# Parity-and-pair order for residuals, results and biases, and a second copy of the first layer's result, in a two-layer hypernetwork convolution

## The chip, the core and the metric

The kernel runs on one core of a Trainium2 chip. The metric is the device time in microseconds of one execution. Before the change it is 4303.06 us, the median of 3 runs (4301.34 to 4310.08). The profile is of one further execution, which took 4305.81 us; its span from the first to the last instruction is 4303.7 us.

## The reference

Two layers of the same form follow each other. Each normalizes its input by groups, computes a weight for every position from a small network on `z`, convolves with it (3 taps), adds a bias from a second network, and adds the input back:

```python
S2, B, CI, CO, L, K, A, H = (32, 32, 64, 64, 256, 3, 16, 128)
h = jax.nn.relu(_ln(z @ W1 + b1, g1, be1))
w = (h @ W2 + b2).reshape(B, L, CI, CO, K)
hb = jax.nn.relu(_ln(z @ Wb1 + bb1, gb1, beb1))
bias = (hb @ Wb2 + bb2).transpose(0, 2, 1)
x_uf = jnp.stack([xp[..., i:i + L] for i in range(K)], axis=-1)
out = jnp.einsum('sbilk,bliok->sbol', x_uf, w) + bias[None]
# twice:
x = x + conv(_gn(x), z, W1, b1, ...)     # x: (32, 32, 64, 256), f32
```

`_gn` splits the last axis (256 positions) into 32 groups of 8 and normalizes over everything but the first axis (32 samples) and the group. So the second layer can't normalize before the first has finished for all 32 images `b`.

## The kernel before, in words

A *unit* `u` is one image `b` of one layer: 0 to 31 are layer 1, 32 to 63 layer 2. A *half* `v = 2u + h` is 32 of its 64 output channels. The main loop runs over the 128 halves.

In a half, `make` (L384) computes twelve pieces of weights, each 16 matmuls `pg <- hT, w2t` (L391, L392); `take` (L395) adds `b2` and moves them into `wall` on DVE (L402) and, for a third of the rows, on ACT (L417). After the first `make` of a half come the `products` (L424) of the half before: 320 short matmuls `pc <- wall, xn` (L434) in four groups `q` of 16 of the 64 positions of a quarter `t`, each group added to the residual by DVE (L443) and, in layer 1, followed by two calls of `bn_stats` (L446) for the next layer's groups. PSUM holds two `pc`. Then `after` (L464) queues what follows a half: `store` of the result, `load_residual` of `v + 2`, `normalize` of half the samples of a coming unit on GpSimd (two steps, L381), the next `load_pairs`, `add_bias` (L362, GpSimd) for `v + 1` and `load_bias` for `v + 2`.

`room` holds `xt`, the buffer for pairs, and `ys`, a ring of three residuals. "Pairs" is the layout that the convolution reads: partition = parity of the position and input channel (2 x 64), free = sample and pair (128). The input `x` lies in DRAM twice: as `xs` (partition = quarter of the positions and sample, 4 x 32; free = output channel and position) for residuals and statistics, and as `xp` in pairs. The first layer's result lies in DRAM once, as `x1[u]`, channel x sample x position. So layer 1 stores each half in four DMAs of 32 partitions, whose contiguous rows are 64 positions, 256 bytes (L368); layer 2 reads residuals in four such DMAs (L144), and reads pairs with all 256 positions: one DMA puts 16 KB rows into partitions 0 to 63 (L132), a second one the same rows shifted by one position into 64 to 127 (L133), and `normalize` takes every other element. In that form `xt` holds only half the samples of a unit, so in layer 2 `next_pairs` (L450) loads the second half of a unit after the first has been normalized, and so on in turn. In layer 1 `xt` holds both halves (`k` = 0, 1).

All these DMAs are issued by SP, in program order; the order is written by hand. Biases are computed in the opening pass (`Hidden.bias`, L225): one ACT instruction (L229) interleaves the parities into position order, and the result goes to `bd` in DRAM, from where `load_bias` spreads a quarter over 32 partitions. The opening pass (`first_stats`, L242) reads all of `xs` for the first statistics (L288). Between the layers `stats` (L302) turns the sums into `gmean` and `rstd`.

## Time and profile before

| | |
|---|---|
| median of 3 runs | 4303.06 us |
| profiled execution | 4305.81 us |
| its span | 4303.7 us |
| mean granted TensorE clock | 0.973 |
| busy: PE, DVE, ACT, POOL | 3955.2, 2637.9, 1294.4, 2083.3 us |
| matmuls of the weights (L391, L392) | 2 x 24576 |
| matmuls of the products (L434) | 40960 |
| DMA: packets, bytes | 637741, 718.48 MB |
| packets under 512 B | 567492 |

The page's digits are busy shares in tenths for 40 equal slices of the span. The opening pass takes about the first 310 us (three slices), layer 1 reaches to about 2210 us, and layer 2 follows:

```profile
PE   5879999999999999999977999899999999899999
...
DMA  8975455454554545545567777777777677677673
```

A row of a view by windows gives a stretch, its length, for each engine its busy time and its number of instructions, then the granted clock, the busy share of the 16 DMA engines and what they moved. In a view of waits an entry is: engine and line that waited, what ended the wait, the sum in us, how often, the longest.

### The profile page before, as it was taken

The page shows a single profiled execution, that of the slowest core. Times are in us where ns is not written, and L with a number is a line of the kernel's source. Part 1 is how long each engine was busy: PE and PEld are TensorE (multiplying, and loading weights), DVE is VectorE, ACT ScalarE, POOL GpSimd, SP SyncE. Part 2 cuts the span into 40 slices and gives each one's busy share as a digit, 9 for nine tenths or more (in the row PEclk, how much of TensorE's full clock was granted, in tenths as well). Part 3 has the DMA queues.
Part 4 walks back from the last instruction along what each step waited for, and adds up shares of the span by engine and source line. Part 5 has one row for each costly group of instructions (what it writes and reads, how often), then busy time and mean ns, then how long its engine had stood idle before and what let it go on. Part 6 is the DMA issues. An engine that isn't in the chain of part 4 may idle for free.

```text
span 4303.7 us, 193876 instructions
## 1 busy us (share of the span) xinstructions
PE 3955.2 (92%) x90704; PEld 3758.3 (87%) x90704; DVE 2637.9 (61%) x3168; ACT 1294.4 (30%) x4264; POOL 2083.3 (48%) x618
## 2 busy tenths in 40 slices
PE   5879999999999999999977999899999999899999
PEld 3559999999999999999977889888888888888898
DVE  6876666666666666666664555555555555555555
ACT  3433233333333333333222223222222222232222
POOL 3456455544555445554425444444544544544542
PEclk8679999999999999999998999999999999999999
DMA  8975455454554545545567777777777677677673
GB/s 309 331 249 167 136 157 145 139 153 138 154 149 135 156 136 153 146 138 153 131 175 169 166 166 174 162 170 172 160 169 175 157 173 177 154 175 175 162 173 98
DMA packets 637741, 718.48 MB, mean 167 GB/s; under 512 B 567492, under 2 KB 583944, under 8 KB 585224
## 3 DMA queue, kind: packets, MB, share of 16 engines
q1 hardware_dynamic: 610824, 692.44, 61.2%
q8 instruction: 709, 11.62, 1.2%
q10 hardware_dynamic: 26112, 13.64, 1.1%
q14 instruction: 96, 0.79, 0.1%
HBM read 559.18 MB, written 146.80 MB: 164 GB/s over the span
## 4 chain that ended last, share of the span: by engine, by line
PE 82%; issue 6%; DVE 6%; DMA 2%; POOL 2%; ACT 1%; SPq 0%; ACTq 0%; POOLq 0%; DVEq 0%
PE pg L391 52%; PE pc L434 23%; PE pg L392 6%; DVE wall L402 3%; POOL sq L199 1%; DMA zt<-in_L_conv_z_dram 1%; DVE parts L446 1%; DVE room L443 1%; PE p L187 1%; POOL xn L381 1%; DMA room<-x 1%; ACT ht L217 0%; ACT sq L191 0%; DMA hd<-ht 0%; DMA xn<-in_xs_dram 0%
## 5 line engine op out<-in xcount | busy, mean ns | idle before, releaser
L391 PE MATMUL pg<-hT,w2t 128*64 128x128 f32 x24576 | 2729.0, 273 | 22.1 <-issue 11.1
L392 PE MATMUL pg<-hT,w2t 128*64 128x128 f32 x24576 | 2729.3, 273 | 11.9 <-issue 11.7
L391 PEld LDWEIGHTS pg<-hT,w2t 128*64 128x64 f32 x24576 | 2677.4, 137 | 45.4 <-DVE wall L402 24.8
L392 PEld LDWEIGHTS pg<-hT,w2t 128*64 128x64 f32 x24576 | 2677.4, 137 | 16.8 <-issue 16.7
L402 DVE TENSOR_TENSOR wall<-pg,b 128x1024 f32<-128x1024 f32 (+1 forms) x1536 | 1864.8, 1220 | 686.1 <-PE pg L392 682.4
L417 ACT ACTIVATE wall<-pg,b 64x128 f32<-64x128 f32 x4096 | 1180.2, 482 | 2800.4 <-DVE wall L402 2004.8
L381 POOL TENSOR_TENSOR xn<-room,gmean 128x2048 f32<-128x2048 f32 x128 | 608.3, 4752 | 1914.6 <-PE pc L434 1620.5
L434 PE MATMUL pc<-wall,xn 128*32 128x128 f32 (+2 forms) x40960 | 1017.5, 255 | 218.0 <-issue 191.0
L434 PEld LDWEIGHTS pc<-wall,xn 128*32 128x32 f32 x40960 | 949.0, 111 | 294.3 <-issue 266.3
L443 DVE TENSOR_TENSOR room<-pc,room 128x512 f32<-128x512 f32 x512 | 354.1, 692 | 903.7 <-PE pc L434 822.0
L381 POOL TENSOR_TENSOR xn<-xn,rstd 128x2048 f32<-128x2048 f32 x128 | 786.2, 6142 | 10.0
L362 POOL TENSOR_TENSOR room<-room,bt 128x2048 f32<-128x2048 f32 x128 | 591.4, 4620 | 79.2 <-DMA bt<-bd 54.1
L446 DVE BATCH_NORM_STATS2 parts<-room 128x6 f32<-128x256 f32 x512 | 192.8, 418 | 8.7
L199 POOL TENSOR_TENSOR sq<-sq 128x512 f32<-128x512 f32 (+2 forms) x192 | 104.0, 542 | 154.4 <-ACT sq L191 141.9
L187 PE MATMUL p<-wc,zt 17*128 17x256 f32 x256 | 94.5, 529 | 38.4 <-DMA zt<-in_L_conv_z_dram 38.4
L187 PEld LDWEIGHTS p<-wc,zt 17*128 17x128 f32 x256 | 64.0, 262 | 59.9 <-issue 38.6
L214 PEld LDWEIGHTS p<-ident,hs 128*128 128x128 f32 x256 | 49.5, 221 | 51.4 <-issue 51.4
L227 PE MATMUL p<-ht,Wb 128*64 128x512 f32 x64 | 58.5, 1014 | 25.4 <-ACT ht L217 25.1
L214 PE MATMUL p<-ident,hs 128*128 128x128 f32 x256 | 60.9, 417 | 3.7 <-DVE hs L205 3.7
L288 DVE BATCH_NORM_STATS2 parts<-xn 128x6 f32<-128x256 f32 x192 | 64.0, 409 | 0.0
L288 DVE BATCH_NORM_STATS2 parts<-room 128x6 f32<-128x256 f32 x160 | 53.5, 411 | 0.0
L288 DVE BATCH_NORM_STATS2 parts<-spare 128x6 f32<-128x256 f32 x160 | 53.5, 409 | 0.0
(44 smaller groups left out, 231.1 us busy)
## 6 DMA issues: line engine op xcount, KB each, us to landing
bt<-bd SPq DMA_DIRECT2D x512, 256.0 KB, 10.2
room<-in_xp_dram SPq DMA_DIRECT2D x64, 1024.0 KB, 9.0
room<-in_xs_dram SPq DMA_DIRECT2D x64, 1024.0 KB, 7.0
x<-room SPq DMA_DIRECT2D x256, 256.0 KB, 4.3
room<-x SPq DMA_DIRECT2D x64, 1024.0 KB, 8.9
room<-x SPq DMA_DIRECT2D x256, 256.0 KB, 6.1
out_dram<-room SPq DMA_DIRECT2D x64, 1024.0 KB, 5.1
room<-x SPq DMA_DIRECT2D x64, 1023.8 KB, 13.2
```

What stands on the lines that cost most here:

```text
L187: nc.tensor.matmul(self.p1[:, k], self.zt[:, k * P : (k + 1) * P], self.t["wc"], start=True, stop=True)
L199: nc.gpsimd.tensor_tensor(to, self.sq[:, :, 0:w], self.sq[:, :, w : 2 * w], ALU.add)
L288: nc.vector.bn_stats(parts[:, g, u, h, :], xv[q % NX][:, j, :, g * E : (g + 1) * E])
L362: nc.gpsimd.tensor_tensor(y, y, bts.pop(v), ALU.add)
L381: nc.gpsimd.tensor_tensor(o, i, b, op)
L391: nc.tensor.matmul(pg[0:C, k, :], w[:, k0 * C : (k0 + 1) * C], h0, start=True, stop=True)
L392: nc.tensor.matmul(pg[C:P, k, :], w[:, k1 * C : (k1 + 1) * C], h1, start=True, stop=True)
L402: nc.vector.tensor_tensor(place(rows, a), pg[rows].rearrange("p o (t m) -> p t m o", t=NT), b2[n][rows, kind, None, None, o0 : o0 + OG].to ...
L417: nc.scalar.activation(place(rows, 0)[:, :, :, k], pg[rows, k].rearrange("p (t m) -> p t m", t=NT), AF.Identity, bias=b2[n][rows, kind, o0 ...
L434: nc.tensor.matmul(pc[t * S : (t + 1) * S, n0 - q * EB : n1 - q * EB, :], xn[:, u % 2, t * MT + p + 1, :], wall[:, t, a : a + (n1 - n0) * CH],
L443: nc.vector.tensor_tensor(part, pc.rearrange("p n o -> p o n"), part, ALU.add)
L446: nc.vector.bn_stats(parts[:, 2 * q + g, u, h, :], part[:, :, g * E : (g + 1) * E])
```

## The change

Within a quarter of the positions, the 64 positions of `xs`, of the residuals and of the output now stand by parity and pair (32 even ones, then 32 odd ones) instead of in position order; the host lays out the input and reads the output so. The bias is stored in that order too, by two ACT instructions in place of one. `products` adds its 16 positions as 8 even and 8 odd ones; `bn_stats` reads runs of 4 of each parity instead of runs of 8.

The first layer's result is stored twice: as `x1` in the layout of a residual (one DMA of 128 partitions, 8 KB rows) and as `x1p` in pairs (eight DMAs of 32 partitions each, rows of 32 pairs of one parity, 128 bytes). Layer 2 reads both with the loads that layer 1 uses for the input: one DMA of 1 MB for a residual, one for a half of the pairs. `xt` then holds both halves in both layers, and `load_pairs` for the next unit follows each `normalize`.

```diff
-    x1 = [dram.tile([C, S, L], FP, name=f"x1_{b}") for b in range(B)]
+    x1 = [dram.tile([NH, P, CH * LT], FP, name=f"x1_{b}") for b in range(B)]
+    x1p = [dram.tile([P, S, M], FP, name=f"x1p_{b}") for b in range(B)]
...
     def load_pairs(u, k):
-        t = pairs(u, k)
-        if u < B:
-            nc.sync.dma_start(out=t, in_=xp[u, k])
-        else:
-            src = x1[u - B][:, k * SH : (k + 1) * SH, :].rearrange("c s l -> c (s l)")
-            t = t.rearrange("p s l -> p (s l)")
-            nc.sync.dma_start(out=t[0:C], in_=src)
-            nc.sync.dma_start(out=t[C:P, 0 : SH * L - 1], in_=src[:, 1 : SH * L])
+        src = xp[u, k] if u < B else x1p[u - B][:, k * SH : (k + 1) * SH, :]
+        nc.sync.dma_start(out=xt[:, k], in_=src)
...
     def load_residual(v):
         u, h = divmod(v, NH)
-        if u < B:
-            nc.sync.dma_start(out=residual(v), in_=xs[:, v])
-        else:
-            for t in range(NT):
-                nc.sync.dma_start(
-                    out=residual(v)[t * S : (t + 1) * S],
-                    in_=x1[u - B][h * CH : (h + 1) * CH, :, t * LT : (t + 1) * LT].rearrange("o s l -> s o l"),
-                )
+        nc.sync.dma_start(out=residual(v), in_=xs[:, v] if u < B else x1[u - B][h])
...
-            bs = self.stage.tile([C, 2, M, 2], FP, tag="bs", name="bs", bufs=2)
-            nc.scalar.activation(
-                bs.rearrange("o b m a -> o b a m"),
-                p3.rearrange("o (b a m) -> o b a m", b=2, a=2),
-                AF.Identity,
-                bias=self.t["bb2"],
-            )
+            bs = self.stage.tile([C, 2, NT, 2, MT], FP, tag="bs", name="bs", bufs=2)
+            for b in range(2):
+                nc.scalar.activation(
+                    bs[:, b],
+                    p3.rearrange("o (b a t m) -> o b t a m", b=2, a=2, t=NT)[:, b],
+                    AF.Identity,
+                    bias=self.t["bb2"],
+                )
...
+    def bn_stats(out, y, g):
+        e = E // 2
+        nc.vector.bn_stats(out, y.rearrange("p o (a m) -> p o a m", a=2)[:, :, :, g * e : (g + 1) * e])
...
         def store(v):
             u, h = divmod(v, NH)
             if u < B:
+                nc.sync.dma_start(out=x1[u][h], in_=residual(v))
                 for t in range(NT):
-                    nc.sync.dma_start(
-                        out=x1[u][h * CH : (h + 1) * CH, :, t * LT : (t + 1) * LT].rearrange("o s l -> s o l"),
-                        in_=residual(v)[t * S : (t + 1) * S],
-                    )
+                    for a in range(2):
+                        nc.sync.dma_start(
+                            out=x1p[u][
+                                a * C + h * CH : a * C + (h + 1) * CH, :, t * MT : (t + 1) * MT
+                            ].rearrange("o s m -> s o m"),
+                            in_=residual(v)[t * S : (t + 1) * S, :, a * MT : (a + 1) * MT],
+                        )
...
-            i = pairs(u, k)[:, :, :: 1 if u < B else 2].rearrange("p s (g e) -> p s g e", g=G)
+            i = xt[:, k].rearrange("p s (g e) -> p s g e", g=G)
...
-                part = y[:, :, q * EB : (q + 1) * EB]
-                nc.vector.tensor_tensor(part, pc.rearrange("p n o -> p o n"), part, ALU.add)
+                eb = EB // 2
+                part = y.rearrange("p o (a m) -> p o a m", a=2)[:, :, :, q * eb : (q + 1) * eb]
+                nc.vector.tensor_tensor(part, pc.rearrange("p (m a) o -> p o a m", a=2), part, ALU.add)
...
             normalize(w, k)
-            if w < B - 1:
+            if w + 1 < U:
                 load_pairs(w + 1, k)
-            elif (w, k) == (B - 1, 1):
-                load_pairs(B, 0)
-            elif w >= B:
-                w, k = divmod(2 * w + k + 1, 2)
-                if w < U:
-                    load_pairs(w, k)
```

The rows below are the program's, in the order in which an engine takes them, without times: line, operation, output and inputs, shape, a count where several equal ones follow each other. `room` is the buffer for pairs and residuals, `bt` the bias, `hT` the hidden vector of a unit. First SP's queue for one unit of layer 1 (two halves), before:

```order
L368 DMA x_2_74<-room 32x32x64 x4
L141 DMA room<-in_xs_dram 128x2048
L128 DMA room<-in_xp_dram 128x2048
L355 DMA bt<-bd_137 32x2048 x4
L368 DMA x_2_74<-room 32x32x64 x4
L141 DMA room<-in_xs_dram 128x2048
L116 DMA hT<-hd_106 128x256
L128 DMA room<-in_xp_dram 128x2048
```

and now:

```order
L355 DMA x_2_74<-room 128x2048
L358 DMA x1p_106<-room 32x32x32 x8
L130 DMA room<-in_xs_dram 128x2048
L123 DMA room<-in_xp_dram 128x2048
L343 DMA bt<-bd_169 32x2048 x4
L355 DMA x_2_74<-room 128x2048
L358 DMA x1p_106<-room 32x32x32 x8
L130 DMA room<-in_xs_dram 128x2048
```

Nine stores stand ahead of the loads of a half where four stood; the loads are the same. Each DMA signals one of eight semaphores in turn, and an issue waits until the one that used its semaphore before has landed, so at most eight of SP's DMAs are under way.

Then SP's queue from the last store of layer 1 to the first two of layer 2 (`out_dram`), before:

```order
L368 DMA x_31_103<-room 32x32x64 x4
L144 DMA room<-x_0_72 32x32x64 x4
L116 DMA hT<-hd_120 128x256
L132 DMA room<-x_0_72 64x4096
L133 DMA room<-x_0_72 64x4095
L132 DMA room<-x_1_73 64x4096
L133 DMA room<-x_1_73 64x4095
L132 DMA room<-x_1_73 64x4096
L133 DMA room<-x_1_73 64x4095
L355 DMA bt<-bd_152 32x2048 x4
L373 DMA out_dram<-room 128x2048
L144 DMA room<-x_1_73 32x32x64 x4
```

and now:

```order
L355 DMA x_31_103<-room 128x2048
L358 DMA x1p_135<-room 32x32x32 x8
L130 DMA room<-x_0_72 128x2048
L118 DMA hT<-hd_152 128x256
L123 DMA room<-x1p_105 128x2048 x2
L123 DMA room<-x1p_106 128x2048
L343 DMA bt<-bd_184 32x2048 x4
L365 DMA out_dram<-room 128x2048
L130 DMA room<-x_1_73 128x2048
L123 DMA room<-x1p_106 128x2048
```

Behind the last store of layer 1, the pairs of the first image (`x_0`) no longer appear: both their halves stand further ahead, beside the stores of image 30. The rows there now are those of the second and third image. The order on PE and on GpSimd is the same row for row; on DVE only the shapes of the evictions change.

More of the change, by code (lines that the diff above doesn't have):

```diff
@@ L82, in conv_layers @@
     room = big.tile([P, SH * L + RING * CH * LT], FP, name="room")
-    xt = room[:, 0 : SH * L]
-    ys = room[:, SH * L :].rearrange("p (r o l) -> p r o l", r=RING, l=LT)
+    xt = room[:, 0 : S * M].rearrange("p (k s m) -> p k s m", k=2, m=M)
+    ys = room[:, S * M :].rearrange("p (r o l) -> p r o l", r=RING, l=LT)
     gmean = const.tile([P, G, S], FP, name="gmean")
@@ L287, in first_stats @@
                 q, j = divmod(v, SV)
-                nc.vector.bn_stats(parts[:, g, u, h, :], xv[q % NX][:, j, :, g * E : (g + 1) * E])
+                bn_stats(parts[:, g, u, h, :], xv[q % NX][:, j], g)
                 if j == SV - 1 and g == GT - 1:
@@ L441, in products @@
                         )
-                part = y[:, :, q * EB : (q + 1) * EB]
-                nc.vector.tensor_tensor(part, pc.rearrange("p n o -> p o n"), part, ALU.add)
+                eb = EB // 2
+                part = y.rearrange("p o (a m) -> p o a m", a=2)[:, :, :, q * eb : (q + 1) * eb]
+                nc.vector.tensor_tensor(part, pc.rearrange("p (m a) o -> p o a m", a=2), part, ALU.add)
                 if u < B:
-                    for g in range(2):
-                        nc.vector.bn_stats(
-                            parts[:, 2 * q + g, u, h, :], part[:, :, g * E : (g + 1) * E]
-                        )
+                    for g in range(2 * q, 2 * q + 2):
+                        bn_stats(parts[:, g, u, h, :], y, g)
         def next_pairs(w, k):
```

13 lines of the change are left out of this document (5 added, 8 removed).

## The prediction

> **What bounds it.** I read the page first, then windows over the two layers, then the chain of waits inside one half-image ("half" below: one v of the loop).
>
> ```profile
> PE 3955.2 (92%) x90704; PEld 3758.3 (87%) x90704; DVE 2637.9 (61%) x3168; ACT 1294.4 (30%) x4264; POOL 2083.3 (48%) x618
> ...
> q8 instruction: 709, 11.62, 1.2%
> ...
> PE 82%; issue 6%; DVE 6%; DMA 2%; POOL 2%; ACT 1%; SPq 0%; ACTq 0%; POOLq 0%; DVEq 0%
> ```
>
> TensorE is the bound, and the second largest entry of the chain is "issue": time in which PE waited for nothing that the profile names. So only what shortens PE's idle time counts. Sixty halves of each layer, from the start of one products call to that of another (columns: stretch, its length, busy time and instructions of PE, PEld, DVE, ACT, POOL, granted clock, DMA share, GB/s):
>
> ```profile
> 378.28:2171.80 1793.52, 1743.82 (x42242) 1695.60 (x42240) 1210.47 (x1440) 560.22 (x1920) 911.24 (x178) 1.00 0.51 146
> 2306.71:4233.13 1926.42, 1755.97 (x42240) 1706.46 (x42240) 1040.34 (x960) 545.73 (x1920) 924.02 (x181) 0.99 0.73 168
> ```
>
> The same 42240 matmuls take 1793.52 us in layer 1 (29.89 a half) and 1926.42 us in layer 2 (32.11 a half), although DVE has less to do there. The clock is nearly the same; the DMA share is 0.51 against 0.73. PE's waits in 390 to 2180 us, then in 2330 to 4200 us:
>
> ```profile
> PE pc L434 <- issue: 36.6, 75, 2.6
> ```
>
> ```profile
> PE pc L434 <- issue: 143.5, 136, 2.8
> ```
>
> The lost time sits in products (L434). The chain there, in one half of layer 2:
>
> ```profile
> 3143.72 2.99 PE pc L434 x125
> 3146.72 0.87 issue
> 3147.59 2.98 PE pc L434 x109
> 3150.57 1.04 issue
> ```
>
> A matmul and its weight load are two instructions; queue q8 carries instructions in packets of 11.62 MB / 709 = 16.4 KB, and 193876 instructions / 709 make 273 a packet, some 130 matmuls. PE runs about that many and stops: it waits for its own code, which the same DMA engines fetch. Products, at 25 ns a matmul (324 in 8.20 us below), eats a packet in 3 us; the makes of a half (384 in 21 us) leave time. Now products and makes of single halves, layer 1, layer 2, and the second to last half, whose loads have run out:
>
> ```profile
> 972.82:981.02 8.20, 7.94 (x324) 7.40 (x324) 4.34 (x9) 0.00 (x0) 8.20 (x2) 1.00 0.02 4
> 981.02:1002.47 21.45, 21.30 (x385) 20.88 (x384) 15.85 (x15) 9.07 (x32) 1.36 (x1) 1.00 0.68 198
> ...
> 3143.65:3153.50 9.85, 7.94 (x323) 7.44 (x324) 2.08 (x3) 0.00 (x0) 0.00 (x0) 1.00 0.14 30
> ...
> 3174.54:3186.02 11.48, 8.18 (x324) 7.47 (x324) 2.07 (x3) 0.00 (x0) 9.66 (x2) 1.00 0.39 88
> ...
> 4233.13:4240.57 7.44, 7.44 (x324) 7.36 (x324) 2.07 (x3) 0.00 (x0) 0.00 (x0) 1.00 0.02 4
> 4240.57:4261.61 21.04, 21.04 (x385) 20.87 (x384) 15.26 (x13) 9.10 (x32) 3.88 (x1) 1.00 0.65 152
> ```
>
> Where no transfer is left over (share 0.02), products takes 7.44 to 8.20 us; where 0.14 x 9.85 = 1.4 us of DMA work is left over, 9.85 (+1.65 on 8.20); where 0.39 x 11.48 = 4.5 us, 11.48 (+3.28). That is the price list for everything below: about 1.2 us of PE for each of the first 1.4 us that the DMA queue runs late, then 0.53 for each more.
>
> **Layer 2: transfers go.** What SP issues there now:
>
> ```profile
> room<-in_xp_dram SPq DMA_DIRECT2D x64, 1024.0 KB, 9.0
> ...
> room<-x SPq DMA_DIRECT2D x64, 1024.0 KB, 8.9
> room<-x SPq DMA_DIRECT2D x256, 256.0 KB, 6.1
> out_dram<-room SPq DMA_DIRECT2D x64, 1024.0 KB, 5.1
> room<-x SPq DMA_DIRECT2D x64, 1023.8 KB, 13.2
> ```
>
> The two pair loads of 1 MB (L132, L133) become one of 1 MB, and the four residual loads in rows of 256 B become one in rows of 8 KB: the very loads of layer 1. So a half of layer 2 then has layer 1's loads, and its products should cost layer 1's mean, 29.89 - 21.45 = 8.44 us, beside its own undisturbed makes of 21.04: 29.48. Gain (32.11 - 29.48) x 60 = **158 us**. Bounds: layer 1's period throughout, (32.11 - 29.89) x 60 = 133; the undisturbed 7.44 + 21.04 = 28.48, 218. GpSimd's first normalize step gains nothing: with the strided input it takes 4.73 us (first row below), as in layer 1.
>
> **Between the layers.** GpSimd and DVE at the seam:
>
> ```profile
> 2227.83 4.73 POOL L381 TENSOR_TENSOR xn<-room,gmean 128x2048 f32<-128x2048 f32 x1 [56.29 <-ACT gmean L331]
> 2232.63 6.25 POOL L381 TENSOR_TENSOR xn<-xn,rstd 128x2048 f32<-128x2048 f32 x1
> 2246.41 4.72 POOL L381 TENSOR_TENSOR xn<-room,gmean 128x2048 f32<-128x2048 f32 x1 [7.52 <-DMA room<-x]
> ...
> 2263.54 4.64 POOL L381 TENSOR_TENSOR xn<-room,gmean 128x2048 f32<-128x2048 f32 x1 [6.56 <-DMA room<-x]
> ```
>
> ```profile
> 2278.51 1.29 DVE L443 TENSOR_TENSOR room<-pc,room 128x512 f32<-128x512 f32 x2 [28.86 <-POOL room L362]
> ```
>
> Three normalize calls and add_bias stand in a row, and DVE's first eviction, so PE, waits for their end. Both halves of the first image are now in SBUF beforehand, and the third load (9.0 us, like xp) is issued after the first step of the first normalize and has two 11 us calls to hide under. The waits of 7.52 and 6.56 go: **-14 us**. Next in line are the three calls themselves; if the loads came late again, 14 is lost.
>
> **Layer 1: stores come.** One store of 1 MB in 8 KB rows is added, and the other goes from 4 x 1024 packets of 256 B to 8 x 1024 of 128 B. DMA after an even half (products end at 1040.65, the next start at 1062.1), then after an odd one (the next start at 1091.8):
>
> ```profile
> 1042.10:1047.30 5.20, 5.00 (x94) 4.76 (x90) 4.26 (x5) 2.27 (x8) 0.00 (x0) 1.00 0.96 225
> 1047.30:1053.00 5.70, 5.70 (x110) 5.70 (x108) 4.09 (x4) 2.27 (x8) 0.00 (x0) 1.00 0.93 355
> 1053.00:1058.00 5.00, 5.00 (x98) 5.00 (x94) 3.46 (x3) 2.27 (x8) 0.00 (x0) 1.00 0.92 200
> 1058.00:1062.10 4.10, 4.10 (x78) 3.94 (x74) 2.66 (x3) 2.27 (x8) 0.00 (x0) 1.00 0.03 12
> ...
> 1083.40:1086.40 3.00, 3.00 (x60) 3.00 (x57) 2.20 (x2) 1.59 (x7) 3.00 (x2) 1.00 0.01 3
> 1086.40:1091.90 5.50, 5.50 (x112) 5.33 (x112) 3.67 (x3) 2.58 (x8) 5.42 (x2) 1.00 0.83 194
> ```
>
> Store, two 8 KB-row loads (2 MB in 5.7 us), bias loads, then 4.1 us free. After the odd half the hole of 3.0 us lies before the bias loads, which wait for add_bias, and their end touches products: that half has only the 3.0. The new 1 MB store costs 5.7 / 2 = 2.9 us. The 8192 small packets are the unknown. The packets of 256 B, in the stretch where one store flows alone:
>
> ```profile
> 1072.00:1074.40 2.40, 2.18 (x40) 1.94 (x38) 2.40 (x3) 1.32 (x6) 2.40 (x1) 1.00 0.74 200
> ```
>
> ```profile
> q1 hardware_dynamic: 1888, 0.48, 73.7%
> ```
>
> That is 200 GB/s and 15 ns of an engine each. The bias loads, 8 KB packets but also 32 partitions at a time, move 200 GB/s too (the stretch from 1053). So bytes over 32 partitions look like the limit, and 1 MB stays at 5.2 us (lower end). If a packet keeps its 15 ns, 8192 / 16 x 15 ns = 7.7 us; if the count is the limit (1888 in 2.4 us), 10.4 us (upper end). I take 6.0, near the byte end, since two unlike transfers show the same rate. Extra DMA time is 2.9 + 0.8 = 3.7 us: the even half hides it (4.1), the odd one runs 0.7 late, 0.8 us of PE, 32 times: **+26 us**.
>
> A sentence of the Trainium skill speaks against this edit: "DMA: Bandwidth & Descriptors", Specifications, asks for 512 B and more for line rate, with a read-modify-write below; its section "Why small descriptors are slow (HBM only)" charges 3 cycles a packet beside a cycle for each 32 B, 7 against 11, so by an estimate from that page 5.2 x 2 x 7/11 = 6.6 us and a sum some 30 us higher. The 256 B row, at 15 ns, already pays such a price; no run here has 128 B.
>
> SP issues nine stores where it issued four:
>
> ```profile
> 1041.43 3.71 SPq L368 DMA_DIRECT2D x<-room  x4
> ```
>
> 0.93 us each, so the residual and pair loads behind them go out some 5 us later; they are used a half later, and the bias loads behind those wait for add_bias or the busy queue anyway. The ninth store and the loads also wait, by the ring of eight semaphores, for the landing of the DMA eight before; the first store lands in 5.1 us (the out_dram row), and seven are queued meanwhile, so the engines do not run dry. Without that cover it is the lateness priced above.
>
> **Shapes.** DVE and ACT by form:
>
> ```profile
> L402 DVE TENSOR_TENSOR wall<-pg,b 128x1024 f32<-128x1024 f32 x1024 | 1248.3, 1223 | 455.7 <-PE pg L392 452.0
> ...
> L443 DVE TENSOR_TENSOR room<-pc,room 128x512 f32<-128x512 f32 x512 | 354.1, 692 | 903.7 <-PE pc L434 822.0 <-DMA bt<-bd 45.8 <-POOL room L362 33.3
> ...
> L446 DVE BATCH_NORM_STATS2 parts<-room 128x6 f32<-128x256 f32 x512 | 192.8, 418 | 8.7
> ...
> L229 ACT ACTIVATE bs<-p,bb 64x512 f32<-64x512 f32 x32 | 23.1, 722 | 26.2 <-PE p L227 23.0 <-DMA bd<-bs 3.2
> ```
>
> The eviction L443 now has runs of 8 where it had 16; L402 has runs of 8 and pays (1223 - 692) / 512 = 1.04 ns an element, so no price shows. Runs of 4 in the statistics are not shown: 0 to 64 x 1.04 = 67 ns a call. In layer 1 DVE's 822 us of waiting for PE cover it; in the opening pass 512 calls could add 34 us. The bias activation becomes two: 0 to 32 x 0.72 = 23 us on ACT, which has 1% of the chain. I take +1 for both, upper end +40.
>
> **Sum.** The profiled execution took 4305.8 us: -158 - 14 + 26 + 1 gives 4161; it is 2.7 above the median shown, so **4158**. Its own range: 4071 (gain 218, small packets free) to 4222 (gain 133, +40).
>
> **Rivals.** (1) Small packets keep 15 ns, 7.7 us: even halves 1.3 late (+1.55), odd ones 2.4 (+2.2), 32 x 3.75 = 120: 4252. For it: over the whole store stretch the engines are 0.96 busy. Against: packets of half the size. (2) The other side: the count is the limit, 10.4 us. Even halves 4.0 late (+3.0), odd 5.1 (+3.6), 32 x 6.6 = 211: 4343, slower. Layer 1 then has layer 2's disease; it outweighs the gain from about 9.2 us on. Against it: equal GB/s of stores and bias loads. (3) The gaps in products are not the queue's doing, and layer 2 keeps 32.11: only the seam, 4290. Against it: 7.44 us in the half without loads, same code, same layer. The Trainium skill, "Runtime: NRT & Kernel Launch", Instruction fetch mechanics, calls the 16 KiB refills mostly hidden and so leans to this rival; the 143.5 us of issue gaps here speak otherwise.
>
> **Chances.** Forecast 0.60, rival 1 0.20, rival 2 0.13, rival 3 0.05, else 0.02. The range 4085 to 4290 leaves out rival 2 and the far end of the gain. A measurement can tell 0.2% (8.6 us) from no change: faster 0.83, same 0.04, slower 0.13.
>
> **What would show it.** Layer 2's sixty halves near 1770 us with DMA share near 0.5; products' issue gaps there as in layer 1 now; no DMA wait of GpSimd at the seam; layer 1's sixty halves near 1820 us, the small stores over by 9 us after their start. Wrong would be layer 1 above 1960 us, or layer 2 above 1850.

## The result, and the profile after

The changed kernel takes **4160.65 us** (median of 4 runs, 4157.90 to 4163.26), the kernel before, on the same chip, 4304.53 us (4301.34 to 4310.08): a ratio of 0.9664, with a 95% interval of 0.9648 to 0.9681. The forecast was 4158 with a range of 4085 to 4290. The profiled execution took 4159.72 us, with a span of 4157.9 us and a granted clock of 0.976.

The page of the changed kernel, the rows that answer those of before (busy times; digits in tenths for 40 slices; the chain that ended last):

```profile
PE 3917.2 (94%) x90704; PEld 3741.3 (90%) x90704; DVE 2642.2 (64%) x3168; ACT 1306.7 (31%) x4296; POOL 2078.0 (50%) x618
...
PE   5879999999999999999997899999999999999999
...
DMA  8966676666666666667667354454444444444442
...
PE 85%; DVE 6%; issue 3%; POOL 2%; DMA 2%; ACT 1%; ACTq 0%; SPq 0%; POOLq 0%; DVEq 0%
```

"issue" went from 6% to 3% of the chain, which is 3% of 4158 us, or some 125 us. The DMA digits have changed sides: 6 and 7 in layer 1, 4 in layer 2. The code (q8) is the same 709 packets, 11.62 MB. Sixty halves of each layer, cut as before (stretch, length, busy time and instructions of PE, PEld, DVE, ACT, POOL, clock, DMA share, GB/s):

```profile
382.10:2224.29 1842.19, 1748.23 (x42243) 1695.48 (x42241) 1211.18 (x1440) 560.10 (x1920) 904.01 (x177) 1.00 0.66 176
2353.37:4086.17 1732.80, 1716.42 (x42243) 1692.31 (x42241) 1040.52 (x960) 554.26 (x1920) 921.38 (x181) 1.00 0.47 150
```

Layer 1 is 48.7 us longer, layer 2 193.6 shorter: layer 2 now takes 28.88 us a half. PE's waits, in 390 to 2220 us and in 2360 to 4080:

```profile
PE pc L426 <- issue: 81.1, 108, 2.4
```

```profile
PE pc L426 <- issue: 12.2, 27, 0.9
```

The gaps in products have nearly left layer 2 (143.5 before) and more than doubled in layer 1 (36.6 before). The chain inside one products call of layer 2 shows one gap where there were gaps after every 110 to 125 entries:

```profile
2958.00 7.30 PE pc L426 x314
2965.30 0.92 issue
2966.22 0.19 PE pc L426
```

Single calls of products, and one half's makes (2966.41), in layer 1 and in layer 2:

```profile
2957.93:2966.41 8.48, 7.56 (x324) 7.23 (x324) 2.08 (x3) 0.00 (x0) 8.48 (x2) 1.00 0.03 7
2966.41:2987.45 21.04, 21.04 (x384) 20.87 (x385) 15.27 (x13) 9.08 (x32) 1.26 (x1) 1.00 0.61 203
3045.02:3052.33 7.31, 7.31 (x324) 7.27 (x324) 2.08 (x3) 0.00 (x0) 0.00 (x0) 1.00 0.02 4
992.28:1001.41 9.13, 7.93 (x324) 7.41 (x324) 4.34 (x9) 0.00 (x0) 9.13 (x2) 1.00 0.10 22
1022.86:1032.99 10.13, 7.88 (x324) 7.45 (x324) 4.33 (x9) 0.00 (x0) 0.00 (x0) 1.00 0.20 46
```

In layer 2 the DMA engines have nothing left when products starts (share 0.02 or 0.03) and some calls have no gap at all: 7.31 us. In layer 1 they still have 0.10 x 9.13 = 0.9 us and 0.20 x 10.13 = 2.0 us of work left in it.

From the starts and ends of all products calls in the traces, means over the sixty halves of a layer. "Left" is the DMA work that was under way in products, per engine; the first number is for even v, the second for odd v:

| | products, us | makes ahead of it, us | left, us |
|---|---|---|---|
| layer 1 before | 8.50 / 8.34 | 21.47 / 21.46 | 0.01 / 0.07 |
| layer 1 after | 9.30 / 9.18 | 21.48 / 21.46 | 0.44 / 1.33 |
| layer 2 before | 10.88 / 10.19 | 21.04 / 22.10 | 4.0 / 1.8 |
| layer 2 after | 7.95 / 7.52 | 21.04 / 21.23 | 0.06 / 0.00 |

Products of an odd v follow the transfers of an even half, and the other way round.

**The seam.** GpSimd between the layers, then DVE's first eviction (start, duration, in brackets the idle time ahead and what ended it):

```profile
2289.08 4.61 POOL L373 TENSOR_TENSOR xn<-room,gmean 128x2048 f32<-128x2048 f32 x1 [58.97 <-ACT gmean L319]
...
2310.84 4.90 POOL L373 TENSOR_TENSOR xn<-room,gmean 128x2048 f32<-128x2048 f32 x1
```

```profile
2326.08 1.29 DVE L436 TENSOR_TENSOR room<-pc,room 128x512 f32<-128x512 f32 x2 [14.92 <-POOL room L350]
```

No normalize waits for a DMA any more. From the first normalize to DVE's eviction it is 37.0 us (2326.08 - 2289.08), where it was 50.7 (2278.51 - 2227.83): 13.7 less. But the stretch from the products of half 62 to those of half 65 lost only 5.7 us (134.8 to 129.1), because the last two calls of layer 1 became longer. Before, then after:

```profile
2171.80:2179.43 7.63, 7.48 (x324) 7.25 (x324) 4.33 (x9) 0.00 (x0) 0.00 (x0) 1.00 0.28 101
2200.90:2210.63 9.73, 7.68 (x322) 7.03 (x320) 4.33 (x9) 0.00 (x0) 0.00 (x0) 1.00 0.24 89
```

```profile
2224.29:2237.67 13.38, 8.99 (x324) 8.55 (x324) 4.33 (x9) 0.00 (x0) 4.54 (x1) 0.90 0.52 206
2259.11:2271.89 12.78, 7.89 (x322) 7.21 (x320) 4.33 (x9) 0.00 (x0) 0.00 (x0) 1.00 0.54 208
```

That is 8.8 us more, with a DMA share of half in both. PE's issue gaps in the two calls are 4.4 and 4.9 us, where they were 0.2 and 2.1; in the first the granted clock was 0.90, too. Layer 2's `w2` weights (8 x 768 KB) are loaded there, and behind the longer row of stores they end later.

**Layer 1's stores.** SP's issues after an even half (start, time that the issues took, count):

```profile
1002.18 0.34 SPq L355 DMA_DIRECT2D x<-room  x1
1002.57 9.99 SPq L358 DMA_DIRECT2D x1p<-room  x8
1012.60 0.70 SPq L130 DMA_DIRECT2D room<-in_xs_dram  x1
```

Windows of the same time: the store in 8 KB rows, the small stores, a hole inside them; last the small stores after the next, odd half:

```profile
1002.70:1005.50 2.80, 2.61 (x48) 2.37 (x46) 2.80 (x4) 1.32 (x6) 0.00 (x0) 1.00 0.94 360
1005.50:1014.00 8.50, 8.50 (x160) 8.50 (x158) 5.71 (x5) 3.21 (x12) 0.00 (x0) 1.00 0.80 132
1007.10:1008.40 1.30, 1.30 (x29) 1.30 (x26) 1.14 (x1) 0.00 (x0) 0.00 (x0) 1.00 0.09 10
...
1036.40:1043.40 7.00, 6.79 (x126) 6.55 (x122) 5.01 (x5) 4.16 (x15) 6.92 (x2) 1.00 1.01 183
```

And the packets of one microsecond in which only small stores flow (1012.5 to 1013.5: packets, MB, time of an engine as a share of 16):

```profile
q1 hardware_dynamic: 1554, 0.20, 118.0%
```

That is 0.20 MB in 1 us, and 16 x 1.18 us / 1554 = 12.1 ns of an engine a packet (a share over 100% means that packets of one engine overlap). While they flow, the small packets move at the 200 GB/s that the forecast put as their lower end. They just don't flow all the time: the third small store in a row takes SP 3.9 us to issue here (1004.24 to 1008.12, the row of SP's timeline between the second and the fourth), and the engines are nearly empty for 1.3 us of it. Over layer 1 that issue takes 3.2 us on average after even halves and 2.2 after odd ones.

**Shapes.** The groups that the change touches (busy, mean ns of one, idle time ahead):

```profile
L436 DVE TENSOR_TENSOR room<-pc,room 128x512 f32<-128x512 f32 x512 | 354.2, 692 | 751.0 <-PE pc L426 629.2
...
L228 DVE BATCH_NORM_STATS2 parts<-room 128x6 f32<-128x256 f32 x672 | 246.4, 416 | 8.7
```

692 ns as before. The second row holds 512 calls in products, which took 418 ns before, and 160 of the opening pass, which took 411: together 416, as now. Runs of 8 and of 4 cost nothing. ACT is busy 12.3 us longer in all (1306.7 against 1294.4).

### The profile page after: what moved, and what is told of

Same layout as the page of the kernel before. It is cut to its first block, busy times and chain, and to the rows that moved or that the text cites. A ratio compares the mean times of both kernels' runs of the same rounds, so it can differ in the third digit from the quotient of the medians.

```text
span 4157.9 us, 194021 instructions
## 1 busy us (share of the span) xinstructions
PE 3917.2 (94%) x90704; PEld 3741.3 (90%) x90704; DVE 2642.2 (64%) x3168; ACT 1306.7 (31%) x4296; POOL 2078.0 (50%) x618
## 3 DMA queue, kind: packets, MB, share of 16 engines
q8 instruction: 709, 11.62, 1.2%
## 4 chain that ended last, share of the span: by engine, by line
PE 85%; DVE 6%; issue 3%; POOL 2%; DMA 2%; ACT 1%; ACTq 0%; SPq 0%; POOLq 0%; DVEq 0%
PE pg L383 54%; PE pc L426 23%; PE pg L384 7%; DVE wall L394 3%; POOL sq L182 1%; DVE parts L228 1%; DVE room L436 1%; DMA bd<-bs 1%; POOL xn L373 1%; ACT ht L200 0%; ACT sq L174 0%; PE p L170 0%; DMA spare<-in_xs_dram 0%; DMA xn<-in_xs_dram 0%; DMA room<-in_xs_dram 0%
## 5 line engine op out<-in xcount | busy, mean ns | idle before, releaser
L384 PE MATMUL pg<-hT,w2t 128*64 128x128 f32 x24576 | 2726.0, 273 | 1.9 <-issue 1.8
L384 PEld LDWEIGHTS pg<-hT,w2t 128*64 128x64 f32 x24576 | 2678.0, 137 | 3.8 <-issue 3.8
L426 PE MATMUL pc<-wall,xn 128*32 128x128 f32 (+2 forms) x40960 | 986.3, 253 | 122.9 <-issue 105.8
L426 PEld LDWEIGHTS pc<-wall,xn 128*32 128x32 f32 x40960 | 934.7, 110 | 181.2 <-issue 164.1
L210 PEld LDWEIGHTS p<-ht,Wb 128*64 128x64 f32 x64 | 8.4, 185 | 47.4 <-ACT ht L200 44.5
```

Source lines behind the costliest of these rows:

```text
L384: nc.tensor.matmul(pg[C:P, k, :], w[:, k1 * C : (k1 + 1) * C], h1, start=True, stop=True)
L426: nc.tensor.matmul(pc[t * S : (t + 1) * S, n0 - q * EB : n1 - q * EB, :], xn[:, u % 2, t * MT + p + 1, :], wall[:, t, a : a + (n1 - n0) * CH],
```

## The experiments

The theory is that of the prediction: PE runs out of code in products, since data transfers hold its code packets up; a half whose queue is empty by then pays nothing. Against it stood that the mere amount of traffic slows PE (wherever it lies), that the gaps are not the queue's doing at all, and for layer 1 that `bn_stats` and not the queue makes its products longer than layer 2's. Each run's time stands beside that of the kernel before on the same chip; where no range is given, it is the time of one execution.

That the gaps are waits for code can be read from the traces themselves. PE has 181408 instructions, matmuls and weight loads, and 181408 / 709 is 256: the packets of q8 carry PE's instructions and no others. (The prediction divided the instructions of all engines and got 273. In the trace a matmul of the program appears twice, each time with a weight load: the 192 in the makes of a half are 384.) And each issue gap of PE in the sixty halves ends 1.2 to 1.7 us after such a packet has landed, all 78 in layer 1 and all 168 in layer 2 of the kernel before, all 115 and all 35 in the changed one. A packet lands only every 5 to 6 us, so this is no accident. In the chain above, a packet landed at 2964.72 and the gap ended at 2966.22. What holds the packets up is the question of the runs.

### One copy more in layer 2, in even or in odd halves

The changed kernel, with one copy of 1 MB from DRAM to DRAM behind the bias loads of every second half of layer 2. In the other run h is 1.

```diff
+    junk = dram.tile([2, P, CH * LT], FP, name="junk")
...
             if v + 2 < NH * U:
                 load_bias(v + 2)
+            if u >= B and h == 0 and u + 1 < U:
+                nc.sync.dma_start(out=junk[u % 2], in_=xs[:, u].rearrange("p o l -> p (o l)"))
```

> The changed kernel with one copy of 1 MB from DRAM to DRAM more behind the loads of each even half of layer 2, where the queue stands empty for about 5 us before the next products. Theory (late queue): the copy ends in time, layer 2's sixty halves stay at 1733 within 10 us. Rival (the amount of traffic: the change took 1 MB a half away and gained 194 us, so half of that comes back with 1 MB in every other half): about 1733 + 95 = 1828, the same as in the run with the copy in odd halves.

> The same copy behind the loads of each odd half of layer 2, where the bias loads end just as the next products starts. Theory (late queue): 2.9 us or more of DMA work is left when products starts, by the price list of the prediction +2.4 us in 30 of the 60 halves, layer 2's sixty halves 1733 + 73 = 1806, by the cheaper price seen in layer 1 of the changed kernel (0.84 us for 1.3 us late) 1790. Rival (the amount of traffic): 1828, the same as with the copy in even halves.

Measured: 4160.59 us with the copy in even halves, 4191.96 in odd ones (4304.95 before). Layer 2's sixty halves and PE's wait in them, first with the copy in even halves:

```profile
2357.78:4086.22 1728.44, 1716.25 (x42243) 1692.66 (x42241) 1040.08 (x960) 552.94 (x1920) 921.07 (x181) 1.00 0.51 168
```

```profile
PE pc L427 <- issue: 8.0, 21, 0.6
```

and in odd halves:

```profile
2358.19:4119.09 1760.90, 1721.94 (x42242) 1692.90 (x42241) 1040.11 (x960) 552.95 (x1920) 918.95 (x181) 1.00 0.51 165
```

```profile
PE pc L427 <- issue: 34.8, 55, 1.8
```

The same bytes and the same DMA share of 0.51 cost nothing after an even half, whose queue has room left, and 32 us more than that after an odd one (28 more than in the changed kernel), whose bias loads wait for add_bias. The amount of traffic, as a cause by itself, falls for this much of it. The place counts, and the time comes as issue gaps in products. The size was overstated: about 2.5 us of DMA work was left in each of the products calls that follow an odd half, and their mean rose to 8.85 us from 7.95, so some 0.4 us for each us of lateness; the price list of the prediction had 1.2 for the first 1.4 us.

### The kernel before, with the pairs read like the input

Only the pair loads are changed: one load of 1 MB for a half of the pairs, both halves in `xt`. Residuals and stores stay as before. (In layer 2 the pairs come from `xp`.)

```diff
-        if u < B:
-            nc.sync.dma_start(out=t, in_=xp[u, k])
-        else:
...
+        nc.sync.dma_start(out=t, in_=xp[u % B, k])
...
-            if w < B - 1:
+            if w + 1 < U:
                 load_pairs(w + 1, k)
-            elif (w, k) == (B - 1, 1):
...
```

> The kernel before, with layer 2's pairs read from the input xp in one load of 1 MB and both halves of a unit in the buffer, as in the changed kernel (the first result's pairs are left out); residuals and stores as before. Theory (late queue): the queue ends some 6.8 us earlier in each half of layer 2 and nothing is left at products: sixty halves from 1926 to about 1745, though the residual keeps its 256 B rows; the seam loses its two DMA waits; layer 1 stays at 1793. Time about 4110. Rival (rows of 256 B are what delays PE's code): at most half of the gain, 1830 or more.

Measured: 4107.95 us (4306.25 before). Layer 2:

```profile
2294.11:4034.51 1740.40, 1720.23 (x42242) 1693.36 (x42240) 1040.47 (x960) 553.06 (x1920) 921.71 (x181) 1.00 0.57 149
```

1926.4 - 1740.4 = 186 of the 193.6 us come from the pair loads alone; products took 7.90 / 7.87 us (even / odd v, here and below). The seam was 120.9 us long, 13.9 less than before: the predicted 14, where no stores were added.

### The kernel before, with the residuals read like the input

```diff
-        if u < B:
-            nc.sync.dma_start(out=residual(v), in_=xs[:, v])
-        else:
...
+        nc.sync.dma_start(out=residual(v), in_=xs[:, v % (NH * B)])
```

> The kernel before, with layer 2's residuals read from the input xs in one load with 8 KB rows (the first result's residual is left out); pairs as before. Same bytes, fewer packets. Theory (late queue): the residual takes about 2.4 us less of the queue, so what is left at products falls from 1.4 and 4.5 us to 0 and about 2: layer 2's sixty halves from 1926 to about 1836, layer 1 unchanged at 1793. Rival (the amount of traffic): the bytes are the same, layer 2 stays at 1926.

Measured: 4339.53 us (4304.95 before), slower. Layer 2, and PE's waits in it:

```profile
2309.02:4266.57 1957.55, 1778.82 (x42243) 1723.95 (x42241) 1040.05 (x960) 543.77 (x1920) 925.84 (x181) 0.99 0.64 165
```

```profile
PE pc L427 <- issue: 65.1, 93, 2.3
PE pg L385 <- issue: 60.0, 39, 2.8
PE pg L384 <- issue: 50.6, 34, 2.8
```

This was the run that neither theory had foreseen. The DMA work goes down (share 0.64 from 0.73), nothing is left when products starts (0.03 / 0.05 us), the products do get shorter (8.67 / 9.43), and still layer 2 takes 31 us more: the gaps are now in the *makes* (L384, L385), 110 us of them, and the makes of a half take 23.83 / 23.36 us. So it can't be only what is left when products starts. The pair loads of before, in rows of 16 KB, now lie wholly beside the makes. A new theory: such long rows hold up code packets wherever they lie, even in makes, which leave time for fetching. The packets' records fit it. How late a packet begins can be counted in PE's instructions, as the number that PE has started beyond 256 for each packet before it: for the packets that begin in the makes of layer 2 it is 354 / 343 on average here, 265 / 277 in the kernel before and 257 / 231 in the changed one.

### The pair loads of before, in rows of 4 KB

The kernel before; each 1 MB pair load is split into four. Bytes and results stay the same.

```diff
-            nc.sync.dma_start(out=t[0:C], in_=src)
-            nc.sync.dma_start(out=t[C:P, 0 : SH * L - 1], in_=src[:, 1 : SH * L])
+            n = SH * L // 4
+            for i in range(4):
+                e = (i + 1) * n - (i == 3)
+                nc.sync.dma_start(out=t[0:C, i * n : (i + 1) * n], in_=src[:, i * n : (i + 1) * n])
+                nc.sync.dma_start(out=t[C:P, i * n : e], in_=src[:, i * n + 1 : e + 1])
```

> The kernel before, with each of the two 1 MB pair loads of layer 2 split into four, so that rows are 4 KB and not 16 KB; same bytes, same order, same results. After the run with the residual as input, in which the queue was shorter and makes got slower, a second theory stands beside the late queue: a code packet waits behind the rows that an engine has already taken in, and rows of 16 KB hold it up longest, in makes too. Theory 2 (long rows): layer 2's sixty halves fall from 1926 to 1850 or less. Theory 1 (late queue alone): the queue's work is the same, 1926 within 15.

and the same split together with the residual of the run above:

> The kernel before, with layer 2's residuals read from the input (left out: the first result's residual) and with the pair loads split into rows of 4 KB: the two earlier edits together. Alone the first made sixty halves of layer 2 slower (1926 to 1958, makes 23.4 and 23.8 us), the second faster (1837). Theory (long rows: a code packet waits behind 16 KB rows wherever PE needs it): without the long rows the shorter queue helps, makes return to 21.1 us and layer 2's sixty halves fall below 1837, to about 1770. Rival (the quick residual itself delays the code, by whatever it moves forward): makes stay at 23 us, 1870 or more.

Measured: 4217.50 us (4306.25 before) for the split alone:

```profile
2307.38:4143.89 1836.51, 1738.00 (x42243) 1695.28 (x42241) 1040.38 (x960) 545.75 (x1920) 923.86 (x181) 1.00 0.72 176
```

```profile
PE pc L437 <- issue: 95.6, 123, 2.1
```

and 4189.08 (4314.33 before) for both:

```profile
2307.76:4115.59 1807.83, 1738.78 (x42242) 1696.73 (x42240) 1040.03 (x960) 544.29 (x1920) 924.68 (x181) 1.00 0.64 178
```

```profile
PE pc L430 <- issue: 60.9, 102, 1.3
PE pg L387 <- issue: 4.3, 11, 0.7
PE pg L388 <- issue: 3.0, 7, 0.6
```

At the same bytes and nearly the same DMA share (0.72), layer 2 loses 90 us when the long rows go: amount falls again, row length counts. And the residual load that cost 31 us with 16 KB rows gains 29 with 4 KB rows; the gaps in the makes go from 110 us to a few, and the makes back to 21.20 / 21.38 us. So it was the long rows that made the run before slower. By the packets' records a row of 16 KB takes its engine 1.2 us, one of 4 KB 0.26 us. (The split also makes four DMAs of each. But the changed kernel has DMAs of 1 MB in rows of 8 KB beside its makes, with 3.1 us of gaps there, so the size of a DMA alone is not the cause; whether the 64 partitions of these loads matter was not tried.) The long rows hold up code in makes too; the lateness comes on top: in the first of the two, 2.63 / 1.24 us are left and products takes 9.48 / 9.47.

One thing stays open: in the second run hardly anything is left (0.15 / 0.10 us), and products still takes 9.20 / 8.48 us, not the 7.5 to 8.0 of the changed kernel. Its DMA share is 0.64 and not 0.47, so in between the amount may count after all: the code packets in its makes begin later than in the changed kernel (329 / 287, counted as above), and products then starts with less code in hand. The 1770 us of the theory were missed by 38.

### Reading the pairs in small rows instead of storing them

The changed kernel without the small stores; layer 2 gathers the pairs from `x1` in 16 loads of 32 partitions, in rows of 128 B. Nothing else is changed.

```diff
-        src = xp[u, k] if u < B else x1p[u - B][:, k * SH : (k + 1) * SH, :]
-        nc.sync.dma_start(out=xt[:, k], in_=src)
...
+        for h in range(NH):
+            src = x1[u - B][h].rearrange("(t s) (o a m) -> t a o s m", t=NT, a=2, m=MT)
+            for a in range(2):
+                p = a * C + h * CH
+                for t in range(NT):
+                    nc.sync.dma_start(
+                        out=xt[p : p + CH, k, :, t * MT : (t + 1) * MT],
+                        in_=src[t][a][:, k * SH : (k + 1) * SH],
+                    )
```

> The changed kernel without the eight small stores; layer 2 reads the pairs straight from x1, the residual's copy, in sixteen loads of 32 partitions with rows of 128 B. Nothing is left out: the small packets move from layer 1's stores to layer 2's loads, where even and odd halves have a free 5 us and a 3 us hole. Theory: layer 1 as in the run without pair stores, 1797; in layer 2 the pairs take 6 to 8 us of the queue in place of 2.7, which the free time hides after one kind of half, and which runs late by up to 2 us after the other: sixty halves from 1733 to 1745 to 1780. Time 4120 to 4145. Rival (reads in 128 B rows cost more than the stores did, as 256 B reads took longer than 256 B stores): layer 2 above 1800, time above 4165.

Measured: 4206.41 us (3 rounds; 4202.33 to 4212.84; 4314.33 before), a ratio of 0.9751, 0.9732 to 0.9771.

```profile
2319.03:4133.59 1814.56, 1732.47 (x42242) 1694.61 (x42240) 1040.05 (x960) 553.18 (x1920) 919.40 (x181) 1.00 0.58 143
```

The rival's figure held. Layer 1 gets 30 us shorter than in the changed kernel (1812.4), layer 2 82 longer. So the small rows are cheaper where the change puts them, in layer 1's stores. It isn't the price of a packet: in the packets' records one of 128 B takes 12.8 ns of an engine on average, in these loads as in the stores. But the row of sixteen loads takes 10.7 / 11.3 us from its first packet to its last (after even / odd halves), where the eight stores take 8.7 / 7.2. What draws it out was not tried.

### Without the small stores

The changed kernel without them; layer 2 reads the pairs of `xp`.

```diff
-        src = xp[u, k] if u < B else x1p[u - B][:, k * SH : (k + 1) * SH, :]
+        src = xp[u % B, k]
...
-                for t in range(NT):
-                    for a in range(2):
-                        nc.sync.dma_start(
...
```

> The changed kernel without the eight small stores of layer 1; layer 2 reads the pairs of the input in their place (the first result's pairs are left out). Theory (late queue: products is slow by the DMA work that is left when it starts, because PE's code comes through the same engines): nothing is late in layer 1 any more, so products there falls to about 7.7 us as in layer 2 of the changed kernel, and sixty halves from 1842 to about 60 x (21.46 + 7.7) = 1750, below the 1793 of the kernel before; layer 2 stays at 1733. Time about 4065. Rival (DVE's statistics make layer 1's products slower, in either kernel): layer 1 returns to 1793 and no further; time about 4110.

Measured: 4106.97 us (4304.95 before). Layer 1, and PE's wait in it:

```profile
386.73:2183.29 1796.56, 1746.36 (x42243) 1695.00 (x42241) 1210.41 (x1440) 558.79 (x1920) 909.72 (x178) 1.00 0.46 146
```

```profile
PE pc L417 <- issue: 28.9, 72, 1.0
```

By this run the small stores cost 1842.2 - 1796.6 = 46 us in layer 1, nearly all of its loss. The run before has the same loads and stores in layer 1, but for its last two halves, and took 1812.4 us there, so by that one it is 30; what makes the 16 us between the two is not known. They also cost the seam: without them it is 119.9 us long, 14.9 less than before, so the 8.8 us in the last two products calls are theirs. But layer 1's products stay at 8.40 / 8.08 us with the DMA share down to 0.46, lower than layer 2's 0.47, and layer 2's take 7.91 / 7.51 in the same run. That spoke for `bn_stats`, which layer 2 lacks, and asked for a run of its own.

### Without the small stores and without the statistics in products

```diff
-                if u < B:
-                    for g in range(2 * q, 2 * q + 2):
-                        bn_stats(parts[:, g, u, h, :], y, g)
```

> The run without pair stores, and without the calls of bn_stats in layer 1's products too (the second layer's statistics are left out). Theory (DVE's statistics make layer 1's products slower): products of layer 1 falls from 8.2 to 7.7 us and makes lose their 0.4 us of waiting for DVE: sixty halves from 1797 to about 1735, as in layer 2. Rival (where the 16 KB packets of code happen to begin): products stays at 8.2, makes lose 0.4: about 1772.

Measured: 4092.77 us (4306.25 before).

```profile
387.90:2170.37 1782.47, 1733.74 (x42243) 1695.63 (x42241) 1040.39 (x960) 552.74 (x1920) 902.99 (x178) 1.00 0.46 147
```

The products do not move (8.51 / 8.23 us); what goes is time in the makes (21.04 / 21.64). The statistics are not what makes layer 1's products longer. What does is open. It could be where the edges of the code packets lie in the calls, which no run here varied. They do lie elsewhere in the two layers: counting what PE takes from its first instruction on, in packets of 256, a call of even v begins 2 to 31 instructions into a packet in layer 1 of the changed kernel and 57 to 86 in layer 2, one of odd v 131 to 160 and 185 to 214. And the changed kernel's first call of all, in layer 1 and with its statistics, has no gap, although the DMA engines are busy for 0.64 of it:

```profile
319.68:326.95 7.27, 7.27 (x324) 7.23 (x324) 4.34 (x9) 0.00 (x0) 7.19 (x3) 1.00 0.64 136
```

So neither the layer nor the work that is left makes a call long by itself; it takes a code packet that is due and is held up.

### The loads of layer 1 between its small stores

The changed kernel; SP issues the large store and two small ones, the residual load, two small ones, the pair load, and the last four.

```diff
-        def store(v):
+        def store(v, part=0):
...
-                for t in range(NT):
+                for t in ((0,), (1,), (2, 3))[part]:
...
                 load_residual(v + 2)
+            if v >= 0:
+                store(v, 1)
...
                 next_pairs(w, k)
+            if v >= 0:
+                store(v, 2)
```

> The changed kernel with the order of a half of layer 1 on SP's queue: large store, two small stores, residual load, two small stores, pair load, four small stores, bias loads. In the changed kernel's trace the engines stand idle for about 2 us a half while SP's issue of a small store takes 1.5 to 3.9 us. Theory (the small stores fill a limited store of descriptors, and a large load between them gives the engines work meanwhile): the queue ends 1.5 to 2 us earlier, products of layer 1 falls by about 0.6 us: sixty halves from 1842 to about 1805, time 4125. Rival (the holes only move, or the loads behind more small stores end as late): 1842 within 8, time 4160.

Measured: 4147.93 us (3 rounds; 4135.90 to 4153.54), a ratio of 0.9634, 0.9607 to 0.9662. SP's issues after one half:

```profile
1001.33 1.62 SPq L359 DMA_DIRECT2D x1p<-room  x2
1002.99 3.87 SPq L130 DMA_DIRECT2D room<-in_xs_dram  x1
1006.91 1.04 SPq L359 DMA_DIRECT2D x1p<-room  x2
1008.04 3.90 SPq L123 DMA_DIRECT2D room<-in_xp_dram  x1
```

The sixty halves of layer 1 take 1831.8 us, which is neither the 1805 of the theory nor the rival's 1842 within 8. The long issue has not gone; it has moved to whatever stands third behind two small stores, here the residual load and then the pair load. A 1 MB load of 128 rows, which takes 0.70 us to issue elsewhere, takes 3.87 there. So it is not the small store itself that takes long to issue; rather, the two stores ahead (1024 packets each) seem to have to get on first. Layer 1's products become 8.05 / 10.08 us, the sum of both 0.35 us less than in the changed kernel. 2.17 us of DMA work is left in both kinds, yet the one is shorter than before the change and the other 1.7 us longer: lateness alone doesn't set the price either; which code packet is due just then may.

### Both versions once more, on one chip

> The changed kernel once more, timed beside the run with loads between the pair stores on one chip. Ratio to the kernel before 0.9664 as first measured, within 0.0015.

> The order with loads between the pair stores once more, beside the changed kernel on one chip. First measured 0.9634 with an interval that touches the changed kernel's; its profile had sixty halves of layer 1 at 1832 against 1842, one kind of half better (8.05 for 9.30 us of products), the other worse (10.08 for 9.18). If that 10 us is real: 0.2 to 0.3% below the changed kernel, with intervals apart; if it is the scatter between runs: the same ratio.

Measured, 5 rounds each: the changed kernel 4156.44 us (4155.51 to 4163.11), a ratio of 0.9693, 0.9674 to 0.9712; with the loads between the stores 4151.99 (4149.86 to 4157.56), 0.9679, 0.9660 to 0.9698. The kernel before ran at 4293.38 here, faster than on the first chip, so the first ratio came out above what was expected of it. The two intervals overlap: the other order gains 7.6 us in layer 1's sixty halves (1843.7 to 1836.1), but by these runs it isn't clearly the better kernel.

## Why the prediction was right, and where it wasn't

The time was right to 3 us, but that is luck: the terms were off by more. In the pieces of the span:

| piece | before, us | after, us | difference | predicted |
|---|---|---|---|---|
| to the third products call | 378.3 | 382.1 | +3.8 | +1 |
| layer 1, sixty halves | 1793.5 | 1842.2 | +48.7 | +24 (26 x 60 / 64) |
| seam | 134.8 | 129.1 | -5.7 | -14 |
| layer 2, sixty halves | 1926.4 | 1732.8 | -193.6 | -158 |
| end | 70.5 | 71.8 | +1.3 | 0 |

Layer 2 gained 36 us more than forecast; layer 1 lost 25 more and the seam gained 8 less. The misses cancel. The mechanism, code that waits behind the transfers, was right.

- **What bounds it: right.** The gaps in products come and go with the data transfers (the copy runs), on the same code, and each ends just after a code packet has landed. So the rival that the gaps are not the queue's doing falls. The Trainium skill ("Runtime: NRT & Kernel Launch", Instruction fetch mechanics) calls the refills mostly hidden; in layer 2 of the kernel before they are not, with 143.5 us of gaps, and in the changed kernel, with 12.2, they nearly are.
- **Layer 2: right cause, mis-sized term.** "Its products should cost layer 1's mean" was the step that failed: they take 7.95 / 7.52 us, not 8.44. Layer 1's products are longer for a reason that is still open (neither its stores nor its statistics). The half without loads in layer 2 itself (7.44 us) was the nearer row. The bounds of 133 and 218 held.
- **The price list: mis-sized.** It was read from layer 2 of before, where 16 KB rows lay in the queue as well, and so it put on lateness what long rows did; its base of 8.20 us was a call of layer 1. By the copies a late us costs some 0.4 us; in layer 1 products got 0.84 us longer for 1.26 us more left after even halves, and 0.80 for 0.43 after odd ones, so one price for all doesn't exist. Nearly half of layer 2's gain (90 of 194 us) could be had by row length alone, of which the prediction had nothing.
- **Layer 1: right price of a packet, wrong time of the row of stores.** 12 ns and 200 GB/s stand at the lower end, as chosen, but the row takes 8.5 and 7.0 us and not 6.0. "The engines do not run dry" was the step that failed: behind two DMAs of 1024 packets the next issue stalls for 3.2 or 2.2 us on average (3.9 in the half shown, with the engines nearly empty for 1.3), although the DMA eight places ahead, whose semaphore it uses, has landed a stage ago. By an estimate from the Trainium skill ("DMA: Bandwidth & Descriptors", Why small descriptors are slow (HBM only)) the row was to take 6.6 us. The rate shows no such price: 197 GB/s for packets of 128 B, 200 for those of 256 B. At 1554 packets a us the 8192 would take 5.3 us, so the rest of the 8.5 and 7.0 is time in which they flow more slowly or not at all. The halves were also the wrong way round: the even ones were to hide it and leave 1.33 us, the odd ones were to be 0.7 late and leave 0.44. Rival 1's lateness (1.3 and 2.4) thus came about in part, at a much lower price than it was given.
- **The seam: right, and something missed.** The two waits of GpSimd went, 13.7 us of 14. What came late next was the `w2` loads of layer 2 behind the longer stores, +8.8 us in the last two products calls of layer 1, which the prediction did not look for.
- **Shapes: right.** No cost in `bn_stats` or the eviction. The opening's +3.8 us says little: over the runs its end lay between 376.9 and 388.3 us.

What stays open: what makes layer 1's products longer than layer 2's, and what makes SP's third issue stall. That the queue holds only so many packets is argued from the runs, not shown; it fits that any DMA is hit there, after 2 x 1024 packets.

## What to carry to other kernels

When an unrolled kernel is bound by TensorE, its shortest matmuls can eat code faster than it is fetched: look for "issue" gaps at even distances in the chain, see what the DMA queues hold just then, and keep that place free of transfers and the loads free of very long rows. Count a split store not only by its packets but by its issues: if two DMAs of some thousand packets stand ahead, whatever is issued third may wait for microseconds. And a price read from a disturbed stretch holds several causes at once, so a clean stretch of the same code is the better base.

## What was not expected of the hardware

- Rows of 16 KB hold up instruction fetches far more than the same bytes in rows of 4 KB: 1926.4 against 1836.5 us for sixty halves, and 110 us of gaps in makes, against 7 us with rows of 4 KB.
- An issue behind two DMAs of 1024 packets took up to 3.9 us, also for a load that takes 0.70 us to issue elsewhere.
- Each stop of PE for code ended 1.2 to 1.7 us after a packet of 256 instructions had landed.
- Stores of 128 B packets over 32 partitions ran at 200 GB/s while they flowed, 12 ns of an engine a packet; the packets of 256 B of before took 15 ns at the same rate. Reading pairs in 128 B rows (sixteen loads) cost 82 us more in layer 2 than loads in 8 KB rows, where the stores cost 30 to 46 us in layer 1.
